# Layer 1's last stage of a two-layer graph and mixture-of-experts kernel: order of the expert-output loads, width of the sums, pieces of the last loads

## The chip, the cores and the metric

The kernel runs on one core of one Trainium2 chip. The metric is the device time of one execution in microseconds (us); of several executions the median is taken. The granted clock of TensorE in the profiled execution was 0.96 of full speed on average.

The engines are named as the profile names them: PE is TensorE's matmul, PEld its weight load, DVE is VectorE, ACT is ScalarE, POOL is GpSimd and SP is SyncE. In this kernel SP computes nothing: it issues most of the plain DMAs, in the order of its queue, and a DMA that has to wait for a semaphore holds all that stands behind it in that queue. POOL issues all indirect DMAs (gathers and scatters of rows).

## The reference, cut to what matters

There are 3327 rows of 256 values. Layer 0 is a graph step and a mixture of 16 experts; layer 1 is a graph step with attention and a mixture of 6 experts. The change lies in the end of layer 1's mixture:

```python
x = x + _L1_gnn_ref(_layernorm(x), adj, L1_gnn_W, L1_gnn_a)
x = x + _L1_ffn_ref(_layernorm(x), ...)

def _L1_ffn_ref(features, ...):
    rh = relu(features @ router_w1 + router_b1)
    expert_logits = softmax(rh @ router_w2 + router_b2)
    top_w, top_i = top_k(expert_logits, 2)
    routing_weights = softmax(top_w)
    h1 = relu(features . expert_w1 + expert_b1)      # 6 experts, 256 x 256
    h2 = relu(h1 . expert_w2 + expert_b2)
    expert_out = h2 . expert_w3 + expert_b3
    sel = take_along_axis(expert_out, top_i)
    return sum(sel * routing_weights[..., None])
```

So every row gets the sum of two weighted expert outputs, and this is added to the row itself.

## The kernel before, in words

The rows are cut into 26 row tiles of 128 rows; four row tiles make a chunk, and there are seven chunks (the last one has two tiles). `xs` holds all rows in SBUF as 128 x 26 x 256. The kernel computes each row only for its two experts. The routing writes, for each expert, a list of its rows into DRAM (`list1`); an entry has three words: the place of the output in `zd`, the number of the row in `hd`, and the weight.

Layer 1's experts are worked off in slots of 256 rows of one expert. There are usually 29 slots, 0 to 28 (`USUAL1`); more are behind a branch (`more`, L545) that is not taken here. `slots1` (L1290) is a software pipeline that Python writes out step by step. In step s it emits, in this order:

- `out1` of slot s-1 (L1254): eight matmuls, then y = acc + bias on DVE (L1262), then two multiplications by the row's weight (L1264), then `rows_out` (L602): two scatters of 128 rows each into `zd`, issued by POOL (L605).
- `weights_of` slot s+2 (L1277): the expert's weights are copied on DVE from `w1_all` into one of three tiles `w1s` (L1281).
- `places` up to slot s+4 (L567): a load of the slot's 256 list entries into `who` by SP (L572). There are 16 `who` tiles.
- `rows_in` up to slot s+3 (L575): two gathers of 128 rows each into `xg`, issued by POOL (L580). There are three `xg` tiles.
- `layer1` of slots s and s+1 (L1240), and `turned` of slot s+2 (L590): the transposes of `xg` on PE (L597).

`zd` has two rows of 256 values for every row: z holds a chunk's part of it as 128 x 4 x 2 x 256. The first four chunks (16 row tiles) are called `LOW`. Slots 0 to 22 (`LATE1` is 23) normally cover all rows of `LOW`; a flag, `early["low"]`, says on the chip whether they do. If so, the loads of z for `LOW` (`results`, L618, the load at L623) can go before the last slots are done; they wait for the scatters of slots 0 to 22 (`z_ready`). Before the change they are emitted one at a time in steps 23 to 26 (L1322), and the sums (`summed`, L629, one operation of 128 x 256 for each row tile and each of the two outputs, L633) and the store into `out` (`stored`, L635, from SP) three steps later (L1324 to L1326). In step 23 the load of z stands ahead of the list load of slot 28, which step 24 emits, because that is the order in which Python writes them.

After the slots come the remaining three chunks, of four, four and two row tiles (L1338 to L1341): one load each from SP, then the sums, and stores issued by ACT. These loads wait for all scatters. The last row tile has 127 rows and is stored in two pieces, 112 and 15 rows (L641).

The order within one engine is that of the program, as a scheduler of the tile framework has laid it out; `tc.issue_after(x)` makes what is in its block stand behind x in the order. `in_order()` (L553) does that for the last `who` load or other SP load of the slots. `last` keeps the instructions that such blocks refer to. DVE, POOL and SP work strictly in that order.

Of the kernel before, what the change touches and what calls it, by code (L numbers as in the profile page):

```python
# [15 lines left out]
OP = mybir.AluOpType  # L16
# [3 lines left out]
P = 128  # L20
# [5 lines left out]
def kernel(  # L26
# [26 lines left out]
    nc = tc.nc  # L53
    N, D = x.shape
    E0, _, H0 = ffn0_w1.shape
    E1, _, H1 = ffn1_w1.shape
# [5 lines left out]
    BT = 4  # L62
    CHUNKS = [list(range(t, min(t + BT, NT))) for t in range(0, NT, BT)]
# [25 lines left out]
    LATE1 = USUAL1 - E1  # L89
    LOW = CHUNKS[: 4 * len(CHUNKS) // 7]  # L90
# [26 lines left out]
    xs = keep.tile([P, NT, D], F32, name="xs")  # L117
# [123 lines left out]
    last = {}  # L241
# [311 lines left out]
    def in_order():  # L553

        return tc.issue_after(last["who"].ins) if "who" in last else nullcontext()

    def expert(table, s, E):

        with in_order():
            return (nc.sync.value_load(table[s : s + 1, 0:1], min_val=0, max_val=E - 1),  # L560
                    nc.sync.value_load(table[s : s + 1, 2:3], min_val=0, max_val=1))

    def load(tile_, source, which):
        e, new = which
        last["who"] = nc.sync.dma_start(tile_, source(bass.ds(e, 1)), cond=new, bounds_check="skip_entire_dma")

    def places(table, s, E, rows_of, size):  # L567

        who = io.tile([P, size // P, 3], I32, name="who", bufs=16)
        with in_order():  # L570
            at = nc.sync.value_load(table[s : s + 1, 1:2], min_val=0, max_val=E * NP)
        last["who"] = nc.sync.dma_start(who, rows_of[bass.ds(at, size), :].rearrange("(h p) w -> p h w", p=P))  # L572
        return who
# [28 lines left out]
    def rows_out(s, who, y):  # L602
        n = who.shape[1]
        for h in range(n):
            last["z"] = nc.gpsimd.indirect_dma_start(  # L605
                out=zviews[n * s + h], out_offset=bass.IndirectOffsetOnAxis(ap=who[:, h, 0:1], axis=0),
                in_=y[:, h, :], in_offset=None, bounds_check=2 * NP - 1, oob_is_err=False,
            )
            if s < LATE1:
                z_ready.append(last["z"].ins.name)  # L610

    def weight(who, h):

        return who.bitcast(F32)[:, h, 2:3]

    z_ready = []

    def results(blk, zp, low=None, z=None):  # L618

        n, t0 = len(blk), blk[0]  # L620
        z = zp.tile([P, BT, 2, D], F32, name="z") if z is None else z
        of, case = (zd, {}) if low is None else (zd_low, dict(cond=low, bounds_check="skip_entire_dma"))
        ins = nc.sync.dma_start(z[:, :n], of[2 * t0 * P : 2 * (t0 + n) * P, :].rearrange("(t p k) d -> p t k d", p=P, k=2), **case)  # L623
        if low is not None:
            for name in z_ready:
                tc.add_manual_dep(ins.ins, name, mybir.DependencyInfo(mybir.DependencyClass.Sync, mybir.DependencyReason.DATA))
        return z

    def summed(blk, z):  # L629

        for i, t in enumerate(blk):
            for k in range(2):
                nc.vector.tensor_tensor(z[:, i, 0, :], z[:, i, k, :], z[:, i, 0, :] if k else xs[:, t, :], op=OP.add)  # L633

    def stored(engine, blk, z):  # L635
        full = [t for t in blk if t < NF]
        engine.dma_start(
            out[full[0] * P : (full[-1] + 1) * P, :].rearrange("(t p) d -> p t d", p=P), z[:, : len(full), 0, :]
        )
# [292 lines left out]
    early = {}  # L932
# [28 lines left out]
    WB, BB = 3 * 2 * H1, 3 * 2 * H1 + D  # L961
# [108 lines left out]
    who = {}  # L1070
# [158 lines left out]
    w1s = [wts.tile([P, BB + 2 * 2], F32, name=f"v_{b}") for b in range(3)]  # L1229
# [7 lines left out]
    def weights1(s, i):  # L1237
        return w1s[s % 3][:, i * 2 * H1 : (i + 1) * 2 * H1].rearrange("p (k h) -> p k h", k=2)
# [15 lines left out]
    def out1(s, who, h2):  # L1254
        ps = bank(1 if s < EARLY1 else 0, [P, 2, D])
        w = weights1(s, 2)
        for h in range(2):
            for c in range(NC1):
                nc.tensor.matmul(ps[:, h, :], h2[:, c, h * P : (h + 1) * P], w[:, c, :],  # L1259
                                 start=(c == 0), stop=(c == NC1 - 1))  # L1260
        y = io.tile([P, 2, D], F32, name="y", bufs=4)
        last["dve"] = nc.vector.tensor_tensor(y, ps, w1s[s % 3][:, None, WB:BB].to_broadcast([P, 2, D]), op=OP.add)  # L1262
        for h in range(2):
            nc.vector.tensor_scalar(y[:, h, :], y[:, h, :], weight(who, h), None, op0=OP.mult)  # L1264
        rows_out(s, who, y)

    who = {}
# [17 lines left out]
    def table1_of(s):  # L1285
        return (early["table"], s) if s < EARLY1 else (table1, s - EARLY1)

    xg, xT, h1, h2, zs = {}, {}, {}, {}, {}

    def slots1(first, end):  # L1290
        for s in range(first - 3, end + 1):
            if first <= s - 1 < end:
                out1(s - 1, who[s - 1], h2.pop(s - 1))
            if first <= s + 2 < end:
                if s + 2 < EARLY1:
                    load(w1s[(s + 2) % 3], lambda e: w1d[e].rearrange("o p w -> p (o w)"), expert(*table1_of(s + 2), E1))
                else:
                    weights_of(s + 2)
            known = EARLY1 if s < EARLY1 - 2 else end
            for i in range(max(who, default=-1) + 1, min(s + 5, known)):  # L1300
                who[i] = places(*table1_of(i), E1, lists[1], S1)
            for i in range(max(xg, default=-1) + 1, min(s + 4, known)):
                xg[i] = rows_in(who[i], hd_of[0][: NE * P, :] if i < EARLY1 else hd[:, :])
            if first <= s < end:
                h2[s] = layer1(s, 1, h1.pop(s))
            if first <= s + 1 < end:
                h1[s + 1] = layer1(s + 1, 0, xT.pop(s + 1))
            if first <= s + 2 < end:
# [68 lines left out]
```

## Time and profile before

| what | value |
|---|---|
| time before, median of 3 runs | 1031.23 us (1025.27, 1031.23 and 1034.23) |
| the profiled execution, its own time | 1030.67 us |
| its span, from the first to the last instruction | 1028.9 us |
| PE busy | 929.3 us (90% of the span) |
| DVE busy | 497.6 us (48%) |
| POOL busy | 428.4 us (42%) |
| ACT busy | 260.8 us (25%) |
| busy PE in the window 954 to 977 us | 23.00 of 23.00 us |
| busy PE in the window 977 to 1003 us | 22.41 of 26.00 us |
| busy PE in the window 1003 to 1029 us | 1.56 of 26.00 us |

The profile is one execution. All times of its rows are counted from the start of the span. A row of the timeline has the start, the duration, the engine, the line of the kernel, the operation, what it writes and reads, how many instructions are merged into the row, and in brackets how long the engine stood idle before it and what ended that. "SPq", "POOLq" and "DVEq" are the sequencers of these engines: the issue of a DMA or a branch, which does not count as busy. A group's row has a count, a total of busy time and the mean of one in ns. The chain of work that ended last is followed back from the last instruction to what released each step.

In the timeline the 29 slots can be told by their y (L1262): those of slots 21 to 28 start at 962.91, 968.58, 974.26, 979.94, 985.62, 994.73, 1000.21 and 1004.63 us. The scatters of slot 22 are the two POOL rows that start at 974.18 and 975.49, those of slot 28 start at 1006.88 and 1008.15.

### The profile page before, as it was taken

The numbers are of one execution on the slowest core, as the hardware profiler recorded it, in microseconds if no ns is written. First come the engines' busy times: TensorE is split into PE (matmuls) and PEld (weight loads), VectorE is DVE, ScalarE is ACT, GpSimd is POOL, SyncE is SP. The second block draws the span as 40 slices with busy tenths as digits, with TensorE's granted clock in tenths as the row PEclk, the third lists the DMA queues.
The fourth block names the chain that finished last, engine by engine and source line by source line (L and its number), as shares of the span: only waits on it lengthen the run. The fifth ranks groups of instructions, "written<-read, shape, count | busy, mean of one in ns | idle before, by whom it ended". The sixth has DMA issues, their size and how long they took to land. (4 is left out here: it accounts for less than half of the span.)

```text
span 1028.9 us, 14333 instructions
## 1 busy us (share of the span) xinstructions
PE 929.3 (90%) x4505; PEld 782.0 (76%) x4505; DVE 497.6 (48%) x1824; ACT 260.8 (25%) x532; POOL 428.4 (42%) x408
## 2 busy tenths in 40 slices
PE   6889999859997999999999989999889588999980
PEld 5678888649886999888898777877668367888870
DVE  6565586225651222212223677658567442344663
ACT  3310302015321111111111443131132333444430
POOL 2040060632575345544544311005242476777741
PEclk9999999969998999999999999999999689999995
DMA  9989678457546575667788398867853955332375
GB/s 338 318 272 307 231 189 305 127 179 236 143 105 189 143 212 149 173 193 185 188 250 236 73 308 288 254 212 181 253 128 129 332 135 151 93 93 93 93 249 195
DMA packets 109634, 204.00 MB, mean 198 GB/s; under 512 B 31843, under 2 KB 64356, under 8 KB 109550
## 3 DMA queue, kind: packets, MB, share of 16 engines
q1 hardware_dynamic: 69952, 154.19, 47.3%
q0 software_dynamic: 20608, 30.69, 13.1%
q10 hardware_dynamic: 18990, 18.14, 5.9%
q8 instruction: 36, 0.59, 0.3%
q14 instruction: 48, 0.39, 0.1%
HBM read 173.74 MB, written 35.53 MB: 203 GB/s over the span
## 5 line engine op out<-in xcount | busy, mean ns | idle before, releaser
L797 PE MATMUL acc<-big,y 128*128 128x512 f32 (+2 forms) x1456 | 341.2, 389 | 28.3 <-DVE big L680 19.8
L797 PEld LDWEIGHTS acc<-big,y 128*128 128x128 f32 (+1 forms) x1456 | 264.3, 193 | 85.7 <-ACT y L853 9.2
L1027 PE MATMUL acc<-xT,w 128*128 128x256 f32 (+3 forms) x1024 | 212.8, 361 | 0.0
L1027 PEld LDWEIGHTS acc<-xT,w 128*128 128x128 f32 x1024 | 186.4, 198 | 15.9 <-issue 3.1
L363 POOL DMA_INDIRECT list<-where,t_idx x104 | 109.3, 1051 | 198.9 <-DVE t_idx L359 87.8
L680 DVE TENSOR_SCALAR big<-adj 128x1536 fp32r<-128x1536 int32 (+6 forms) x130 | 111.5, 860 | 121.3 <-DMA adj<-in_adj_t 78.2
L1056 POOL DMA_INDIRECT xd<-y,who x64 | 99.0, 1547 | 65.2 <-DVE y L1055 19.2
L1050 PE MATMUL acc<-w,hid 128*128 128x256 f32 (+3 forms) x512 | 118.0, 381 | 0.7 <-DVE x_out L439 0.7
L1002 POOL DMA_INDIRECT xg<-hd,who x64 | 63.2, 988 | 123.2 <-PE acc L1027 44.2
L1035 DVE TENSOR_TENSOR hid<-hid,acc 128x512 f32<-128x512 f32 (+3 forms) x64 | 40.1, 629 | 139.7 <-PE acc L1027 134.1
L1050 PEld LDWEIGHTS acc<-w,hid 128*128 128x128 f32 (+3 forms) x512 | 89.5, 178 | 20.7 <-issue 3.3
L1031 ACT ACTIVATE hid<-acc 128x512 f32<-128x512 f32 (+3 forms) x64 | 35.2, 550 | 202.6 <-PE acc L1027 195.9
L605 POOL DMA_INDIRECT zd<-y,who x58 | 70.2, 1210 | 25.2 <-DVE y L1264 14.3
L1250 ACT ACTIVATE h<-acc,v 128x256 f32<-128x256 f32 x116 | 55.0, 475 | 100.3 <-PE acc L1247 99.3
L580 POOL DMA_INDIRECT xg<-hd,who x58 | 57.9, 999 | 31.8 <-issue 15.8
L1247 PE MATMUL acc<-xT,v 128*128 128x256 f32 x232 | 63.5, 397 | 4.4 <-DMA v<-w1d 3.9
L1055 DVE TENSOR_SCALAR y<-acc,who 128x256 f32<-128x256 f32 x64 | 28.1, 478 | 71.7 <-PE acc L1050 68.0
L1262 DVE TENSOR_TENSOR y<-acc,v 128x512 f32<-128x512 f32 x29 | 20.1, 692 | 86.8 <-PE acc L1259 86.8
L1247 PE MATMUL acc<-h,v 128*128 128x256 f32 x232 | 61.3, 387 | 0.6 <-ACT h L1250 0.6
L268 POOL TENSOR_TENSOR ln_var<-ln_var,half 128x2 f32<-128x2 f32 (+2 forms) x19 | 15.2, 802 | 104.5 <-DVE ln_var L266 92.2
L1259 PE MATMUL acc<-v,h 128*128 128x256 f32 x232 | 56.7, 387 | 0.1
L1247 PEld LDWEIGHTS acc<-xT,v 128*128 128x128 f32 x232 | 44.6, 203 | 13.3 <-issue 4.2
(281 smaller groups left out, 926.7 us busy)
## 6 DMA issues: line engine op xcount, KB each, us to landing
adj<-in_adj_t SPq DMA_DIRECT2D x66, 768.0 KB, 6.4
w<-in_ffn_w SPq DMA_DIRECT2D x72, 512.0 KB, 5.8
adj<-in_adj_t SPq DMA_DIRECT2D x25, 639.5 KB, 6.0
adj<-in_adj_t SPq DMA_DIRECT2D x25, 512.0 KB, 4.3
v<-w1d SPq DMA_DIRECT2D x7, 898.0 KB, 10.5
hd<-ln_h ACTq DMA_DIRECT2D x12, 512.0 KB, 10.6
z<-zd SPq DMA_DIRECT2D x6, 1024.0 KB, 8.1
w_all<-w1d SPq DMA_DIRECT2D x6, 898.0 KB, 12.7
```

The lines of the kernel that those rows point to most:

```text
L363: ins = nc.gpsimd.indirect_dma_start(out=rows_of[2 * (t0 + j) + i], out_offset=bass.IndirectOffsetOnAxis(ap=idx[:, i, j : j + 1], axis=0), ...
L580: last["pool"] = nc.gpsimd.indirect_dma_start(out=xg[:, h, :], out_offset=None, in_=of, in_offset=bass.IndirectOffsetOnAxis(ap=who[:, h, 1 ...
L605: last["z"] = nc.gpsimd.indirect_dma_start(out=zviews[n * s + h], out_offset=bass.IndirectOffsetOnAxis(ap=who[:, h, 0:1], axis=0), in_=y[: ...
L680: last["mask"] = nc.vector.tensor_scalar(mask[:kr, :, :cols], a[:kr, :, :cols], value, None, op0=op)
L797: last["graph"] = nc.tensor.matmul(acc[c][k][:, :w], y[:kr, j, part, k * P : (k + 1) * P], mask[:kr, jj, i0 : i0 + w], start=(j == 0 and p ...
L1002: last["pool"] = nc.gpsimd.indirect_dma_start(out=xg[:m, h, :], out_offset=None, in_=hd_of[0][: NE0 * P, :] if s < HALF else hd[:, :], in_ ...
L1027: last["slot"] = nc.tensor.matmul(q[:, c, :n], w[:, k, h0 : h0 + 2 * P - 1 : 2], xT[:, k, :n], start=(k == 0), stop=(k == KD - 1))
L1050: nc.tensor.matmul(ps[:m, h, :], hid[c // 2][:, c % 2, h * P : h * P + m], w3[:, c // 2, c % 2, :], start=(c == 0), stop=(c == NC0 - 1))
L1056: ins = nc.gpsimd.indirect_dma_start(out=xd_of[2 + h] if s < USUAL0 else xd, out_offset=bass.IndirectOffsetOnAxis(ap=who[s][:m, h, 0:1], a ...
L1247: ins = nc.tensor.matmul(ps[:, c, :], w[:, k, c : H1 : NC1], src[:, k, :], start=(k == 0), stop=(k == 1))
L1250: last["act"] = nc.scalar.activation(dst[:, c, :], ps[:, c, :], AF.Relu, bias=w1s[s % 3][:, BB + 2 * i + c : BB + 2 * i + c + 1])
L1259: nc.tensor.matmul(ps[:, h, :], h2[:, c, h * P : (h + 1) * P], w[:, c, :], start=(c == 0), stop=(c == NC1 - 1))
```

## The change

It has three parts. All of them lie in the end of layer 1; two line offsets follow from it (L623 becomes L625, L633 becomes L635, L1262 becomes L1265).

1. The loads of z for `LOW` are emitted as two in step 24 and two in step 25, and not before the list load of slot 28. Each also waits for the y of the step's `out1` (`behind`), that is, for the last multiplication of slot 23's y (first two loads) and slot 24's (last two). `last["dve"]` is now that multiplication and not the addition before it.
2. A chunk's sums are two operations of 128 x 1024 and not eight of 128 x 256: first z's output 0 plus `xs`, then output 1 plus that. They are emitted for chunk 0 in step 25, for chunk 1 in step 26 and for chunks 2 and 3 in step 27, behind the weight copy and the y of that step.
3. The last three chunks are loaded, summed and stored in five pieces of two row tiles each, so the sums there are of 128 x 512.

On the engines the order changes as follows. SP's queue: the list load of slot 28 now stands right behind that of slot 27, and the four loads of z come behind it without anything between them. POOL's: the two gathers of slot 28 now stand ahead of the two scatters of slot 23, where they stood behind them; earlier, the scatters of slot 4 move ahead of the first gather of slot 8. DVE's: y of slot 24, weights of 27, sums of chunk 0, y of slot 25, weights of 28, sums of chunk 1, y of slot 26, sums of chunks 2 and 3, y of slots 27 and 28, and then the ten sums of the last pieces. Before, the sums of `LOW` were spread between the weight copy of slot 28 and y of slot 28. ACT's: seven stores at the end and not five. PE's order is the same.

```diff
-    def results(blk, zp, low=None, z=None):
-
-        n, t0 = len(blk), blk[0]
+    def results(blk, zp, low=None, z=None, behind=(), step=BT):
         z = zp.tile([P, BT, 2, D], F32, name="z") if z is None else z
         of, case = (zd, {}) if low is None else (zd_low, dict(cond=low, bounds_check="skip_entire_dma"))
-        ins = nc.sync.dma_start(z[:, :n], of[2 * t0 * P : 2 * (t0 + n) * P, :].rearrange("(t p k) d -> p t k d", p=P, k=2), **case)
-        if low is not None:
-            for name in z_ready:
-                tc.add_manual_dep(ins.ins, name, mybir.DependencyInfo(mybir.DependencyClass.Sync, mybir.DependencyReason.DATA))
+        for i in range(0, len(blk), step):
+            part = blk[i : i + step]
+            n, t0 = len(part), part[0]
+            ins = nc.sync.dma_start(z[:, i : i + n], of[2 * t0 * P : 2 * (t0 + n) * P, :].rearrange("(t p k) d -> p t k d", p=P, k=2), **case)
+            if low is not None:
+                for name in (*z_ready, *behind):
+                    tc.add_manual_dep(ins.ins, name, mybir.DependencyInfo(mybir.DependencyClass.Sync, mybir.DependencyReason.DATA))
         return z
 
     def summed(blk, z):
 
-        for i, t in enumerate(blk):
-            for k in range(2):
-                nc.vector.tensor_tensor(z[:, i, 0, :], z[:, i, k, :], z[:, i, 0, :] if k else xs[:, t, :], op=OP.add)
+        n, t0 = len(blk), blk[0]
+        for k in range(2):
+            nc.vector.tensor_tensor(z[:, :n, 0, :], z[:, :n, k, :], z[:, :n, 0, :] if k else xs[:, t0 : t0 + n, :], op=OP.add)
...
-        last["dve"] = nc.vector.tensor_tensor(y, ps, w1s[s % 3][:, None, WB:BB].to_broadcast([P, 2, D]), op=OP.add)
+        nc.vector.tensor_tensor(y, ps, w1s[s % 3][:, None, WB:BB].to_broadcast([P, 2, D]), op=OP.add)
         for h in range(2):
-            nc.vector.tensor_scalar(y[:, h, :], y[:, h, :], weight(who, h), None, op0=OP.mult)
+            last["dve"] = nc.vector.tensor_scalar(y[:, h, :], y[:, h, :], weight(who, h), None, op0=OP.mult)
         rows_out(s, who, y)
...
-            if not first and 0 <= s - LATE1 < len(LOW):
-                results(LOW[s - LATE1], tail, early["low"], zs[s - LATE1])
-            if not first and 0 <= s - LATE1 - 3 < len(LOW):
-                with tc.issue_after(last["copy"].ins):
-                    summed(LOW[s - LATE1 - 3], zs[s - LATE1 - 3])
-                stored(nc.sync, LOW[s - LATE1 - 3], zs.pop(s - LATE1 - 3))
-
+            for i in LOADED.get(s - LATE1, ()) if not first else ():
+                with in_order():
+                    results(LOW[i], tail, early["low"], zs[i], [last["dve"].ins.name])
+            for i in SUMMED.get(s - LATE1, ()) if not first else ():
+                with tc.issue_after(last["copy"].ins), tc.issue_after(last["dve"].ins):
+                    summed(LOW[i], zs[i])
+                stored(nc.sync, LOW[i], zs.pop(i))
+
+    LOADED, SUMMED = {1: (0, 1), 2: (2, 3)}, {2: (0,), 3: (1,), 4: (2, 3)}
...
-    zs = [(blk, results(blk, tail)) for blk in CHUNKS[len(LOW) :]]
+    zs = [(blk, results(blk, tail, step=2)) for blk in CHUNKS[len(LOW) :]]
     for blk, z in zs:
-        summed(blk, z)
-        stored(nc.scalar, blk, z)
+        for i in range(0, len(blk), 2):
+            summed(blk[i : i + 2], z[:, i : i + 2])
+            stored(nc.scalar, blk[i : i + 2], z[:, i : i + 2])
```

More of the change, by code (lines that the diff above doesn't have):

```diff
@@ L616 @@
     z_ready = []
-    def results(blk, zp, low=None, z=None):
-        n, t0 = len(blk), blk[0]
+    def results(blk, zp, low=None, z=None, behind=(), step=BT):
         z = zp.tile([P, BT, 2, D], F32, name="z") if z is None else z
         of, case = (zd, {}) if low is None else (zd_low, dict(cond=low, bounds_check="skip_entire_dma"))
-        ins = nc.sync.dma_start(z[:, :n], of[2 * t0 * P : 2 * (t0 + n) * P, :].rearrange("(t p k) d -> p t k d", p=P, k=2), **case)
-        if low is not None:
-            for name in z_ready:
-                tc.add_manual_dep(ins.ins, name, mybir.DependencyInfo(mybir.DependencyClass.Sync, mybir.DependencyReason.DATA))
+        for i in range(0, len(blk), step):
[5 more added lines that the diff above has]
+                    tc.add_manual_dep(ins.ins, name, mybir.DependencyInfo(mybir.DependencyClass.Sync, mybir.DependencyReason.DATA))
         return z
     def summed(blk, z):
-        for i, t in enumerate(blk):
-            for k in range(2):
-                nc.vector.tensor_tensor(z[:, i, 0, :], z[:, i, k, :], z[:, i, 0, :] if k else xs[:, t, :], op=OP.add)
+        n, t0 = len(blk), blk[0]
+        for k in range(2):
+            nc.vector.tensor_tensor(z[:, :n, 0, :], z[:, :n, k, :], z[:, :n, 0, :] if k else xs[:, t0 : t0 + n, :], op=OP.add)
     def stored(engine, blk, z):
         full = [t for t in blk if t < NF]
-        engine.dma_start(
-            out[full[0] * P : (full[-1] + 1) * P, :].rearrange("(t p) d -> p t d", p=P), z[:, : len(full), 0, :]
-        )
+        if full:
+            engine.dma_start(
+                out[full[0] * P : (full[-1] + 1) * P, :].rearrange("(t p) d -> p t d", p=P), z[:, : len(full), 0, :]
+            )
         for lo, hi in last_rows() if blk[-1] >= NF else ():
@@ L1320, in slots1 @@
                 early["more"] = asked(*table1_of(USUAL1))
-            if not first and 0 <= s - LATE1 < len(LOW):
-                results(LOW[s - LATE1], tail, early["low"], zs[s - LATE1])
-            if not first and 0 <= s - LATE1 - 3 < len(LOW):
-                with tc.issue_after(last["copy"].ins):
-                    summed(LOW[s - LATE1 - 3], zs[s - LATE1 - 3])
-                stored(nc.sync, LOW[s - LATE1 - 3], zs.pop(s - LATE1 - 3))
+            for i in LOADED.get(s - LATE1, ()) if not first else ():
[6 more added lines that the diff above has]
+    LOADED, SUMMED = {1: (0, 1), 2: (2, 3)}, {2: (0,), 3: (1,), 4: (2, 3)}
+    assert len(LOW) == 4 and max(SUMMED) < E1
     tail = ctx.enter_context(tc.tile_pool(name="tail", bufs=len(CHUNKS)))
```

## The prediction

> **What bounds the kernel now.** I read the windows first: PE is busy 23.00 of 23.00 us from 954 to 977, 22.41 of 26.00 from 977 to 1003 and 1.56 of 26.00 after that. So PE's work bounds the slots until 977; then something makes PE wait, and behind 1003 a chain without PE sets the end. The change touches only these two stretches (50 us). The waits of 975 to 1029 us name what PE lacked:
>
> ```profile
> POOL xg L580 <- DMA who<-list: 5.6, 1, 5.6
> PE mm L597 <- DMA xg<-hd,who: 2.9, 2, 2.5
> ```
>
> Columns: total us, times, longest. The list load of slot 28 comes late, so do its gathers, so PE stands 2.9 us. The timeline shows why:
>
> ```profile
> 977.30 0.98 POOL L605 DMA_INDIRECT zd<-y,who  x1 [0.30 <-issue]
> 978.58 0.97 POOL L605 DMA_INDIRECT zd<-y,who  x1 [0.30 <-issue]
> 978.64 0.37 SPq L623 DMA_DIRECT2D z<-zd  x1
> 979.27 0.37 SPq L572 DMA_DIRECT2D who<-list  x1
> ...
> 980.05 2.34 SPq L623 DMA_DIRECT2D z<-zd  x3
> ...
> 985.15 0.98 POOL L580 DMA_INDIRECT xg<-hd,who  x1 [5.59 <-DMA who<-list]
> ...
> 991.55 0.48 PE L597 MATMUL mm<-ident,xg 128*128 128x128 f32 x2 [2.49 <-DMA xg<-hd,who]
> ```
>
> The list load stood in SP's queue behind the first z load, which waited for slot 22's scatters, and then behind its 1024 KB in the DMA queue. y of slot 25 starts at 985.62 and y of slot 26 at 994.73: 9.11 us, where the slots before take 5.68 each. The loss is 3.43 us.
>
> A second loss, in POOL's rows near the end:
>
> ```profile
> 1001.78 3.51 POOL L605 DMA_INDIRECT zd<-y,who  x1 [2.98 <-DVE y L1264]
> ...
> 1005.60 0.97 POOL L605 DMA_INDIRECT zd<-y,who  x1 [0.31 <-DVE y L1262]
> 1006.88 0.97 POOL L605 DMA_INDIRECT zd<-y,who  x1 [0.30 <-issue]
> 1008.15 0.98 POOL L605 DMA_INDIRECT zd<-y,who  x1 [0.31 <-issue]
> ```
>
> Slot 27's first scatter takes 3.51 us against 0.97; the three after it queue up. The chain that ended last then goes through the last scatter and the last z loads:
>
> ```profile
> 1008.15 3.75 DMA zd<-y,who
> ...
> 1012.24 5.94 DMA z<-zd
> ...
> 1018.27 2.64 DVE z L633 x8
> 1020.96 2.17 DVE z L633 x7
> ```
>
> From 1018.27 DVE sums without a pause to 1025.07; a load that is out at 1012.24 lands 5.94 us later.
>
> **The change part by part.** The sum is made against the profiled execution: span 1028.9, own time 1030.67, 0.56 under the median 1031.23.
>
> *1. The list load ahead of the z loads.* Slot 28's list load follows slot 27's, which was out before 940 (SP's rows from 940 on begin with the z load at 978.64). The buffer it refills is slot 12's, long done. Its gathers stand on POOL behind slot 22's scatters, so at 977.30 and 978.58, 7.85 us earlier; with 2.8 us to land (the DMA page's median near there) they are there by 982.4, and PE asks at 988.9. The stall goes: -3.43 us. y's operands from slot 26 on are ready at 991.3, 996.5 and 1001.2. Slot 23's scatters go 2.6 us later; no early z load waits for them, the last loads wait for far later ones, and POOL, with no more gathers to issue, has caught up by slot 25. Earlier, slot 4's scatters pass slot 8's first gather (866.63 to 869.19); its second gather stays at 870.49 and PE takes both at 875.25 without a wait: nothing.
>
> *2. The z loads.* SP holds the first for slot 22's scatters as before: 978.64. Slot 23's y, the added wait, ended at 975.6: nothing. The second follows 0.5 to 1 us later; the last two wait for slot 24's y, 981.28, and went out near 981 and 982 before. Behind them in SP's queue are only the stores. So the landings stay, about 984.3 (before the list load behind it, which POOL had by 985.15), 987.25 (980.05 and 7.2 us to landing), 990 (between), 993.7 (982 and 11.7).
>
> *3. The wide sums.* No row has 128x1024. A 128x256 addition takes 421 ns alone and every 0.337 us in a row (6.73 us for 20 in 1018 to 1025); y's 128x512 takes 692 ns. The slope is 271 ns for 256, so I estimate 1.23 us for 1024. The second of a pair must wait for the first (before, another tile stood between), so a chunk costs 2.5 us against 2.7: bounds 2.2 (full overlap) and 2.7 (no gain). DVE's new order, with what waits:
> - sums 0 stand behind slot 27's weight copy (ends 982.6), wait for the first landing, 984.3, and end at 986.8. Queued behind are slot 25's y (ready 985.62, ends 988.2) and slot 28's weight copy (ends 989.5). PE needs that copy at 992.0 (995.39 in the timeline, less 3.43): 2.5 us to spare.
> - sums 1: 989.5 to 992.0. y 26: ready 991.3, ends 993.4.
> - sums 2 and 3: the last landing 993.7; four operations, end about 998.1. y 27, ready 996.5, ends 999.5; y 28 starts when ready, at 1001.2.
> So each y from 25 to 27 is late, by 0.7 to 1.6 us; their scatters have time, and the late sums are no longer beside slot 27's scatter.
>
> *4. POOL's end.* Slot 27's scatters run from about 999.5 to 1001.7, so slot 28's start as soon as weighted: 1001.2 + 0.73 + 0.35 + 0.28 = 1002.55, the second at 1003.83 instead of 1008.15. That is 4.32 us with the 3.43 in it, so the queue gives 0.89. The bound below: the 3.51 comes again on slot 27, 2.54 us, and slot 28's second scatter starts at about 1005.9; then this part and the first give 2.2 in all.
>
> [...]
>
> *5. The pieces.* Counted from the first z load's issue: before, 1024 KB land at 5.94, the next at 8.6 (12.73 and 8.1 later), the last 512 KB, by the GB/s of 2 us windows (45, 325, 330, 384, 227), at about 9.95. The same rates put the first 512 KB at 4.35 (adj's 512.0 KB loads: 4.3), the others at 5.95, 7.3, 8.6, 9.95. A piece's sums are two dependent 128x512: 2 x 0.69 + 0.08 = 1.46 against 1.35. DVE runs 4.45 to 5.9, then from 6.05 on without a pause: four pieces, to 11.9, against 12.83: -0.9. Then ACT's stores: before, the 128-row store was issued ahead of the last sums (1024.77 against 1025.07); now all three come behind: +0.45. Net -0.5. The two more loads and stores are issued (0.4 us each) beside the sums. Bounds: -1.1 (overlapped sums) and +0.95 (first piece no earlier than 5.94).
>
> Sum: -3.43 - 0.89 - 0.5 = -4.8 us. Own time 1025.9, span 1024.1, against the median 1031.23: **1026.4**. The bounds of the parts give -1.3 (2.2 less 0.95) to -5.4 (4.32 and 1.1).
>
> **The rivals.**
> - *DVE or POOL takes up half of it.* The last early landing comes 3.5 us later (997.2, so that y 27 ends at 1002 and its scatters push slot 28's), or a scatter of slot 27 is held like that at 1001.78: either way slot 28's second scatter starts 2.1 us later, at 1005.9. For it: the 3.51 us row, which the profile doesn't explain. Against: only one such row, and DVE has nothing left to do beside slot 27's scatters. 1026.4 + 2.1 = 1028.5.
> - *Slower: sums 0 hold DVE.* Place: slot 25's y and slot 28's weight copy wait behind a z load. With a landing at T the copy ends at T + 5.2 and PE pays from T = 986.8 on; at 986.8 + 4.8 = 991.6 all is eaten. If the loads share the queue so that all land with the last, at 993.7, it costs 6.9: 1033.3. For it: four loads are in flight together. Against: they landed one after another, 987.25 to 993.7, and POOL had the small load behind the first by 985.15.
> - *Pieces that don't overlap.* Five loads of 4.3 us in a row take 21.5 where 9.95 did: about 11.5 slower, 1038. The landings of before overlap, 2.7 us apart for 1024 KB, and speak against it. [...]
> - *It doesn't do what it says:* slot 28's gathers come no earlier, 1031. The order on SP and POOL speaks against it.
>
> **How the numbers follow.** Forecast 0.65 (its own range 1024 to 1028, before the scatter of runs); half of it 0.18; sums hold DVE 0.07; serial pieces 0.03; nothing 0.04; more than the sum, 1020 to 1024, 0.03. The three runs before spread over 9 us, so a median of three may lie 2.5 us off. The range is 1021.5 to 1031.5: it holds forecast, half and nothing with that scatter and leaves out the slower rivals. A measurement of this kernel can tell about 1% (10.3 us) from no change. Faster by over 1% needs less than 1020.9: 0.06, from the scatter and the last case. Slower by over 1% needs more than 1041.5: 0.03. Within 1%: 0.91.
>
> **What would show it.** No wait of PE for xg near 989 and 5.7 us between the y of slots 25 and 26; slot 28's gathers at 977.3; sums 0 before y 25; no scatter over 1.6 us behind 999; the second scatter of slot 28 near 1003.8; first piece landed 4.3 us after its issue, DVE done 11.9 after it. I am wrong if slot 28's weight copy makes PE wait, if y 28 starts later than its operands, or if the pieces land together.

## The result, and the profile after

| what | before | after |
|---|---|---|
| median, 20 runs each | 1030.74 us | 1021.68 us |
| lowest and highest of them | 1019.63 to 1038.19 | 1014.14 to 1028.81 |
| the profiled execution, its own time and span | 1030.67, 1028.9 | 1028.81, 1026.3 |
| start of slot 22's y in it | 968.58 | 972.25 |

The ratio of the times is 0.9935, with a 95% interval from 0.9906 to 0.9964. Of 1030.74 us that is 6.7 us less, from 3.7 to 9.7; the two medians themselves lie 9.06 us apart. The forecast was 4.8 us less.

Two executions of one and the same kernel reach slot 22 up to 16 us apart (three profiles of before: 955.61, 968.58, 971.38), for reasons upstream of the change. The profiled execution of after is also the slowest of its 20. So single spans can't be compared. In what follows I use **the stretch**: from the start of slot 22's y to the start of the last instruction that the profile shows, 0.05 us before the end of the span. It is 60.26 us in the profile of before and 53.97 in that of after; a second profile of after and one of its variant without pacing (e7 below) gave 54.01 both.

The waits after 975 us, in the profile after (columns: total us, times, longest):

```profile
DVE z L635 <- DMA z<-zd: 11.7, 2, 9.3
POOL zd L605 <- DVE y L1267: 8.1, 6, 3.5
...
PE acc L1250 <- ACT h L1253: 0.6, 1, 0.6
```

PE's wait for `xg` and POOL's for `who` are gone from the list. The timeline after, for SP, POOL, DVE and PE:

```profile
980.96 0.98 POOL L580 DMA_INDIRECT xg<-hd,who  x1 [0.30 <-issue]
982.24 0.98 POOL L580 DMA_INDIRECT xg<-hd,who  x1 [0.30 <-issue]
982.32 3.67 SPq L625 DMA_DIRECT2D z<-zd  x4
...
988.78 1.23 DVE L635 TENSOR_TENSOR z<-z,xs 128x1024 f32<-128x1024 f32 x1 [2.48 <-DMA z<-zd]
990.04 1.23 DVE L635 TENSOR_TENSOR z<-z 128x1024 f32<-128x1024 f32 x1
991.19 0.68 DVE L1265 TENSOR_TENSOR y<-acc,v 128x512 f32<-128x512 f32 x1
...
992.56 0.64 PE L597 MATMUL mm<-ident,xg 128*128 128x128 f32 x4
992.72 1.09 DVE L1284 COPY v<-w_all 128x1796 f32 x1 [0.20 <-issue]
...
997.37 2.35 DVE L635 TENSOR_TENSOR z<-z,xs 128x1024 f32<-128x1024 f32 x2
997.47 1.96 POOL L605 DMA_INDIRECT zd<-y,who  x1 [1.68 <-DVE y L1267]
999.74 1.96 POOL L605 DMA_INDIRECT zd<-y,who  x1 [0.30 <-DVE z L635]
...
1003.26 0.97 POOL L605 DMA_INDIRECT zd<-y,who  x1 [1.56 <-DVE y L1267]
...
1007.49 0.98 POOL L605 DMA_INDIRECT zd<-y,who  x1 [0.30 <-issue]
1011.57 2.45 SPq L625 DMA_DIRECT2D z<-zd  x5
```

Slot 28's gathers go out at 980.96 and 982.24, which is 8.7 and 10.0 us behind slot 22's y; before it was 16.6 and 17.9. PE transposes them at 992.56 without a wait. Chunk 0's sums stand ahead of slot 25's y, which starts at once behind them, and slot 28's weight copy (992.72) ends at 993.81; PE uses it at 995.62, so 1.8 us are to spare. Slot 26's scatters (997.47, 999.74) take 1.96 us each beside the wide sums, but POOL then stands idle for 1.56 us before slot 27's, so that is absorbed. The chain that ended last now reads (start, us, what):

```profile
1007.49 3.75 DMA zd<-y,who
...
1011.57 3.80 DMA z<-zd
...
1015.47 0.70 DVE z L635
...
1021.61 0.69 DVE z L635
```

It goes through the same steps, but the first piece lands 3.80 us after its issue and DVE is done 10.73 us after it (12.83 before).

One part of this chain is not what its name says. The rows of the last scatter have landed at 1009.78, 2.29 us after its start (2.29 before, too). The rest of its 3.75 us goes to the branch `more` (L549) that is not taken: POOL waits there for its own scatters and then spends 1.24 us in one instruction, to 1011.30, and the trace has the semaphores that SP's loads wait for set near the end of it, by 1011.25:

```profile
L549 POOLq INC_SWDGE_SEM x1: 1235/1235/1235, 1010.1 to 1010.1; - x1
```

The change leaves this part alone, so the third column of the next table is the same in nearly all rows.

### The profile page after: what moved, and what is told of

Same layout as the page of the kernel before. It is cut to its first block, busy times and chain, and to the rows that moved or that the text cites. A ratio compares the mean times of both kernels' runs of the same rounds, so it can differ in the third digit from the quotient of the medians.

```text
span 1026.3 us, 14305 instructions
## 1 busy us (share of the span) xinstructions
PE 930.8 (91%) x4505; PEld 783.3 (76%) x4505; DVE 495.9 (48%) x1790; ACT 260.6 (25%) x532; POOL 429.9 (42%) x408
## 5 line engine op out<-in xcount | busy, mean ns | idle before, releaser
L1053 PEld LDWEIGHTS acc<-w,hid 128*128 128x128 f32 (+3 forms) x512 | 89.6, 178 | 19.6 <-issue 3.3
L605 POOL DMA_INDIRECT zd<-y,who x58 | 70.4, 1214 | 26.7 <-DVE y L1267 16.6
L1265 DVE TENSOR_TENSOR y<-acc,v 128x512 f32<-128x512 f32 x29 | 20.0, 691 | 80.7 <-PE acc L1262 77.6
L1262 PE MATMUL acc<-v,h 128*128 128x256 f32 x232 | 56.3, 385 | 0.1
```

What stands on the lines that cost most here:

```text
L605: last["z"] = nc.gpsimd.indirect_dma_start(out=zviews[n * s + h], out_offset=bass.IndirectOffsetOnAxis(ap=who[:, h, 0:1], axis=0), in_=y[: ...
L1053: nc.tensor.matmul(ps[:m, h, :], hid[c // 2][:, c % 2, h * P : h * P + m], w3[:, c // 2, c % 2, :], start=(c == 0), stop=(c == NC0 - 1))
```

## The experiments

Each row is one profiled execution, cut at four marks: slot 28's y, its second scatter, the first of the last z loads, and the end of the stretch. All are in us, the first column from the start of slot 22's y. The rows without an e are the two kernels.

| kernel | y 28 | to its 2nd scatter | to the last loads | to the end | stretch |
|---|---|---|---|---|---|
| before | 36.05 | 3.52 | 4.08 | 16.61 | 60.26 |
| e11_before_again | 40.36 | 2.63 | 4.08 | 16.49 | 63.56 |
| e13_before_third | 35.16 | 3.52 | 4.09 | 16.63 | 59.40 |
| after | 32.61 | 2.63 | 4.08 | 14.65 | 53.97 |
| e12_after_again | 32.61 | 2.74 | 4.08 | 14.58 | 54.01 |
| e4_list_first | 32.61 | 5.05 | 4.08 | 16.44 | 58.18 |
| e1_loads_only | 32.61 | 5.04 | 4.08 | 16.53 | 58.26 |
| e2_wide_only | 38.76 | 2.63 | 4.09 | 16.31 | 61.79 |
| e3_pieces_only | 36.87 | 3.52 | 4.08 | 14.59 | 59.06 |
| e5_narrow | 33.77 | 3.93 | 4.09 | 14.21 | 56.00 |
| e7_no_pace | 32.62 | 2.63 | 4.08 | 14.68 | 54.01 |
| e8_sums_last | 32.62 | 3.62 | 7.07 | 15.46 | 58.77 |
| e9_ones | 32.62 | 2.63 | 4.08 | 14.31 | 53.64 |
| e10_zero_last | 39.60 | 5.18 | 4.09 | 14.49 | 63.36 |

My theory was that of the prediction: the position of slot 28's list load makes PE wait, the long scatter costs at POOL's end, the pieces shorten the last stretch. The rivals: the pacing or the wide sums do it, the sums hold DVE, or the pieces don't overlap.

**e4_list_first: the old kernel, only slot 28's list load one step earlier.**

```diff
-            for i in range(max(who, default=-1) + 1, min(s + 5, known)):
+            for i in range(max(who, default=-1) + 1, min(s + (6 if first == 0 and s == LATE1 else 5), known)):
```

> The kernel before with one edit: the list load of slot 28 stands ahead of the first z load in SP's queue. Loads of z, sums and tail as before. I read the end stretch, from the start of slot 22's y to the end of the span: 60.3 us before, 54.1 after the change. Theory (the list load behind the z load is the cause of PE's stall, and the change gains 3.4 us by it, 0.9 in POOL's queue and 1.9 in the last pieces): PE's wait for xg is gone, slot 27's and 28's y are ready 3.4 us earlier, the stretch is 56.0 to 56.9. Rival (the stall comes from the z loads' traffic on the DMA queues, which the change paces): the wait stays at least in half, the stretch is over 58.5.

Measured: stretch 58.18. PE's wait is gone and y 28 stands where after has it, 3.44 us earlier than in the profile of before. So the order of these two loads on SP is the cause of the stall; this step of the theory stands. But the stretch lies 1.3 us above the range expected. POOL's timeline in e4 tells why:

```profile
996.15 4.86 POOL L605 DMA_INDIRECT zd<-y,who  x1 [3.31 <-DVE y L1264]
1001.31 3.84 POOL L605 DMA_INDIRECT zd<-y,who  x1 [0.30 <-DVE z L633]
1005.45 1.01 POOL L605 DMA_INDIRECT zd<-y,who  x1 [0.31 <-DVE y L1264]
```

Both scatters of slot 26 are held beside the narrow sums, 4.86 and 3.84 us where 0.97 is usual. Those of slots 27 and 28 queue up behind them, and slot 28's second starts 5.05 us after its y where after needs 2.63. Of the 3.44 us that PE gained, 1.5 (5.05 less 3.52) are lost again at POOL.

**e1_loads_only: part 1 alone** (`results` with `behind`, the loads in steps 24 and 25, `last["dve"]` moved; the sums narrow and in their old steps, the last loads whole).

```diff
-            if not first and 0 <= s - LATE1 < len(LOW):
-                results(LOW[s - LATE1], tail, early["low"], zs[s - LATE1])
+            for i in {1: (0, 1), 2: (2, 3)}.get(s - LATE1, ()) if not first else ():
+                with in_order():
+                    results(LOW[i], tail, early["low"], zs[i], [last["dve"].ins.name])
```

> Part 1 of the change alone: the z loads of the first four chunks as in the change (behind all list loads, two by two, paced by y), sums narrow and at their old steps, the last three chunks whole. Theory: as with the list load moved alone, the end stretch 56.0 to 56.9 us. Rival (pacing the loads by y is worth something of its own): under 55.5; or (it costs, since the loads are later) over 57.5.

Measured: 58.26, and missed in the same way: slot 26's scatters took 4.52 and 4.17 us. The number lies in the range of the rival that the later loads cost something, but e4, which doesn't pace them, agrees within 0.09 us in every column. So in this stretch what part 1 does is the order on SP's queue, and the pacing shows no effect.

**e2_wide_only: part 2 alone** (`summed` as in the change, in the old steps).

```diff
-        for i, t in enumerate(blk):
-            for k in range(2):
-                nc.vector.tensor_tensor(z[:, i, 0, :], z[:, i, k, :], z[:, i, 0, :] if k else xs[:, t, :], op=OP.add)
+        n, t0 = len(blk), blk[0]
+        for k in range(2):
+            nc.vector.tensor_tensor(z[:, :n, 0, :], z[:, :n, k, :], z[:, :n, 0, :] if k else xs[:, t0 : t0 + n, :], op=OP.add)
```

> Part 2 alone: the kernel before with a chunk's sums as two operations. Theory: PE's stall stays (2.9 us of waiting for xg), the last chunks' sums take 6.2 us instead of 6.7, and slot 27's first scatter is held by one wide sum at most (about 2 us instead of 3.5): end stretch 58.5 to 60.3. [...]

Measured: 61.79, more than expected, but for a reason that isn't the sums: y 28 came at 38.76, since the granted clock fell to 0.5 behind PE's wait (see e11). No scatter took over 1.97 us, where about 2 were expected at most. Behind y 28 the last part is 16.31, against 16.49 to 16.63 in the three profiles of before. The 2.63 to the second scatter alone shows nothing: e11, with narrow sums, has the same. POOL's timeline of e2:

```profile
985.26 1.96 POOL L605 DMA_INDIRECT zd<-y,who  x1 [0.31 <-DVE z L633]
...
994.75 1.96 POOL L605 DMA_INDIRECT zd<-y,who  x1 [4.98 <-DVE y L1264]
997.02 1.97 POOL L605 DMA_INDIRECT zd<-y,who  x1 [0.31 <-DVE z L633]
```

The three scatters beside wide sums took 1.96 or 1.97 us, and none took more.

**e3_pieces_only: part 3 alone** (five pieces, their sums narrow).

```diff
-    zs = [(blk, results(blk, tail)) for blk in CHUNKS[len(LOW) :]]
+    zs = [(blk, results(blk, tail, step=2)) for blk in CHUNKS[len(LOW) :]]
```

> Part 3 alone: the kernel before with the last three chunks loaded, summed and stored in five pieces, sums narrow. Theory: the first piece lands 3.8 us after the first issue instead of 5.9, the end comes 1.5 to 2.1 us earlier, the end stretch is 58.2 to 58.8. Rival (pieces gain nothing, the gain there came from the wide sums): 59.8 to 60.8.

Measured: 59.06, above the 58.2 to 58.8 expected, again with the clock fallen for 3.4 us (y 28 at 36.87, 0.8 later than in before). The last part is 14.59 against 16.61: the pieces alone give 2.0 us, four times what was predicted for them, and the wide sums add nothing to it there (14.65 in after). If anything they cost a little in the last part: with narrow sums it is 14.59 here and 14.21 in e5.

**e5_narrow: the changed kernel with narrow sums.**

> The change with narrow sums (128x256) in the same places of DVE's order. New theory, after the list load moved alone gave only 2.1 of 3.4 us (slot 26's scatters took 4.86 and 3.84 us beside runs of narrow sums): a scatter that starts just after a sum is held until the run of sums ends, and wide sums let it in after one. Expected: slot 26's first scatter, which starts beside the 16 narrow sums of chunks 2 and 3, takes 3 to 6 us; the end stretch (from slot 22's y to the end, 54.0 after the change) is 54.5 to 57. Rival (the width is nothing, the change's order of sums alone frees the scatters): no scatter over 2.1 us, stretch 53.7 to 54.3.

Its edit puts the removed lines of e2's diff back. Measured: 56.00, inside the expected size, but not by the mechanism: no scatter was held for long here, as the rival had it. POOL's timeline of e5:

```profile
988.16 1.16 POOL L605 DMA_INDIRECT zd<-y,who  x1 [2.44 <-DVE y L1267]
989.63 1.04 POOL L605 DMA_INDIRECT zd<-y,who  x1 [0.30 <-issue]
994.78 0.97 POOL L605 DMA_INDIRECT zd<-y,who  x1 [4.11 <-DVE y L1267]
```

Instead POOL waited 4.11 us for slot 27's weighted rows: the first z load went out 1.3 us later than in after (11.37 against 10.07), and the sixteen narrow sums of chunks 2 and 3 (5.4 us) stand ahead of slot 27's y, which started at 32.52 instead of 29.67. So y 28 came 1.16 later too. The later load isn't due to the edit: e11, the kernel before, has the same 11.37. The landings tell the two causes apart. From the landing of chunk 0 DVE works almost without a pause to slot 27's y, and that takes 13.15 us in after, e12 and e9, though chunk 0 landed at 16.52, 16.94 and 16.79 there; in e5 it landed at 17.97 and the same work took 14.55. So of the 2.85 us by which slot 27's y came later, 1.45 are the landing and 1.40 the narrow sums.

**e8_sums_last: the changed kernel with the sums of chunks 2 and 3 behind slot 28's y.**

```diff
-    LOADED, SUMMED = {1: (0, 1), 2: (2, 3)}, {2: (0,), 3: (1,), 4: (2, 3)}
+    LOADED, SUMMED = {1: (0, 1), 2: (2, 3)}, {2: (0,), 3: (1,), 6: (2, 3)}
```

> The change with the sums of chunks 2 and 3 behind slot 28's y instead of ahead of slot 27's. Theory (scatters are held beside sums): slot 26's and 27's scatters take 0.97 to 1.1 us, slot 27's y is no longer late, but slot 28's two scatters now stand beside wide sums and take about 2 us each, so the last z loads start 1 to 2 us later than after the change: stretch 55 to 56. Rival (scatters are held by something else, the sums only happen to be near): slot 28's scatters take 0.97, stretch 53.7 to 54.3.

Measured: 58.77, well above 55 to 56. The scatters of slot 28 were held as the theory said; from the timeline of e8:

```profile
993.27 1.97 POOL L605 DMA_INDIRECT zd<-y,who  x1 [2.45 <-DVE y L1267]
995.54 1.96 POOL L605 DMA_INDIRECT zd<-y,who  x1 [0.30 <-DVE z L635]
996.68 1.51 SPq L640 DMA_DIRECT2D out_x<-z  x2
1002.60 2.49 SPq L625 DMA_DIRECT2D z<-zd  x5
```

That costs 1.0 us up to the second scatter's start. But the last loads then go out 7.07 us later instead of 4.08, of which the second scatter's own hold is 1.0. The other 2 us weren't in the expectation. The trace shows what they are made of. The second scatter landed 4.51 us after its start instead of 2.29. Of these 2.2 us its hold is 1.0; why the other 1.2 came is not shown, but the two stores into `out` were in flight beside it. And SP, which stands at the branch L549 ahead of the loads, waits there for the semaphores of these two stores. SP's waits in e8 from 990 to 1004 us have the row:

```profile
SPq L549 <- SPq L549: 3.5, 3, 2.1
```

The longest of these waits ends at 1001.88, when the second store (out at 997.82) has landed. POOL had set its semaphores by 1001.52, so SP's wait costs 0.8 us. The sums of `LOW` have no good place behind slot 28's y.

**e10_zero_last: the changed kernel with chunk 0 loaded last, its sums still ahead of slot 25's y.** This tests the slower rival.

```diff
-    LOADED, SUMMED = {1: (0, 1), 2: (2, 3)}, {2: (0,), 3: (1,), 4: (2, 3)}
+    LOADED, SUMMED = {1: (1, 2), 2: (3, 0)}, {2: (0,), 3: (1,), 4: (2, 3)}
...
-        nc.vector.tensor_tensor(y, ps, w1s[s % 3][:, None, WB:BB].to_broadcast([P, 2, D]), op=OP.add)
+        with tc.issue_after(last["sum"].ins) if "sum" in last else nullcontext():
+            nc.vector.tensor_tensor(y, ps, w1s[s % 3][:, None, WB:BB].to_broadcast([P, 2, D]), op=OP.add)
```

> The change with chunk 0 loaded as the last of the first four chunks, and its sums kept ahead of slot 25's y as in the change. It tests the slower rival of the prediction: DVE held by a z load that lands late. Theory: chunk 0 lands at 25.2 us after slot 22's y, slot 28's weight copy ends at about 30.3, PE needs it at 23.4, PE waits 6.5 to 7.5 us; the stretch is 60 to 63 (longer if TensorE's clock drops after the wait). Rival (DVE's lateness is covered elsewhere): under 57.

Measured: 63.36. The timeline of e10:

```profile
991.92 1.23 DVE L635 TENSOR_TENSOR z<-z,xs 128x1024 f32<-128x1024 f32 x1 [10.32 <-DMA z<-zd]
...
994.33 0.68 DVE L1266 TENSOR_TENSOR y<-acc,v 128x512 f32<-128x512 f32 x1
...
995.07 2.08 PE L1262 MATMUL acc<-v,h 128*128 128x256 f32 x4 [2.45 <-DVE y L1266]
...
997.00 1.36 PEld L1250 LDWEIGHTS acc<-xT,v 128*128 128x128 f32 x4 [0.58 <-DVE v L1285]
```

DVE stands for 10.32 us before the load, and PE stands behind DVE's y and then its weight load behind the weight copy. Slot 28's copy ends at 29.57 instead of 21.57 us after slot 22's y; PE had 1.8 us to spare, so 6.2 us should reach it. It used the copy 6.25 later, and y 28 came 7.0 later, with the clock at half for 6.8 us in between. The mechanism of the rival is real; it didn't come about because the loads land one after another (at 16.52, 19.64, 22.50 and 25.17 us in after). The 5.18 us behind y 28 is a side effect of the edit: slot 27's weighting came behind slot 28's addition on DVE (its scatter started at 40.83).

**e11_before_again and e13_before_third: the kernel before, unchanged, profiled twice more.**

> The kernel before, unchanged, for one more profile. In the profiles of part 2 alone and part 3 alone TensorE's granted clock fell to 0.5 for 6.8 and 3.4 us right behind PE's wait for slot 28's rows, which lengthened these stretches by 2.7 and 0.8 us; in the profile of before it did not fall there. Theory (that fall follows the wait in some executions, so on average the change gains more than 3.4 us by taking the wait away): the stretch is 60.3 without a fall and 61 to 63.5 with one. Rival (the fall belongs to those two kernels): 60.1 to 60.5 and no fall.

> The kernel before, for a third profile. Theory (PE's wait for slot 28's rows is there each time, a fall of the granted clock right behind it most times): stretch 60.3 without a fall, 61 to 63.6 with one.

Measured: 63.56 and 59.40. The stall is no constant: y 28 stands at 36.05, 40.36 and 35.16 in the three profiles. It follows the list load of slot 28, which went out at 10.69, 12.00 and 9.89; so e13 stayed below the 60.3 expected without a fall of the clock. In e11 PE stood 4.21 us, and then its matmuls ran slowly. The timeline of e11, and the row of the windows that holds it (the last three columns are granted clock, DMA share and GB/s):

```profile
980.29 0.67 PE L597 MATMUL mm<-ident,xg 128*128 128x128 f32 x2 [4.21 <-DMA xg<-hd,who]
981.54 0.70 PE L597 MATMUL mm<-ident,xg 128*128 128x128 f32 x2 [0.57 <-DMA xg<-hd,who]
982.03 3.62 PE L1259 MATMUL acc<-v,h 128*128 128x256 f32 x8
```

```profile
980.00:985.00 5.00, 4.14 (x11) 3.14 (x12) 0.00 (x0) 0.59 (x1) 1.81 (x2) 0.50 0.60 218
```

The profile of before has the same eight matmuls behind its stall, in 1.89 us:

```profile
992.80 1.89 PE L1259 MATMUL acc<-v,h 128*128 128x256 f32 x8
```

The granted clock fell to 0.5 for 3.4 us (e3) or 6.8 us (e2, e10, e11) near the end of PE's waits or right behind them, in four of the six profiles that have such a wait. In this stretch it stayed at 1.00 in before and e13 until PE's work was done. Of the eight profiles without such a wait, that of after shows 1.00 in all windows from 940 to 1005 us, and y 28 stands at 32.61 or 32.62 us in seven. The length of the waits alone doesn't tell the two cases apart: in before PE waited 2.49 and 0.43 us and the clock stayed; in e3 it waited only 1.02 and 1.08 us, with a pair of transposes between, and the clock fell:

```profile
984.25 0.48 PE L597 MATMUL mm<-ident,xg 128*128 128x128 f32 x2 [1.02 <-DMA xg<-hd,who]
985.80 0.70 PE L597 MATMUL mm<-ident,xg 128*128 128x128 f32 x2 [1.08 <-DMA xg<-hd,who]
```

In e13 the waits were 1.03 and 1.00 us and it didn't fall. What decides stays open.

**e12_after_again and e7_no_pace: the changed kernel again, and without the wait for y.**

```diff
-                for name in (*z_ready, *behind):
+                for name in z_ready:
```

> The change, unchanged, for one more profile. Theory (without PE's wait nothing in the stretch depends on the clock's fall, and the scatters of slots 27 and 28 stand beside no sums): the stretch is 53.5 to 54.6 again. Rival (the stretch after the change varies as before's did, 60.3 and 63.6): outside of that.

> The change without the added wait of the z loads for y. Theory (the pace is neutral): the last two of the four loads are issued about 1 us earlier, sums 2 and 3 end no later, slot 28's y starts when its operands are ready: stretch 53.5 to 54.6. Rival (the pace keeps the z loads out of the gathers' way): PE waits for slot 28's rows, stretch over 55.

Measured: 54.01 and 54.01. After repeats within 0.04, where the three profiles of before differ by 4.2. Without the pacing the four loads go out at 9.28, 9.97, 10.65 and 11.60, and nothing that counts moves; it costs nothing and gives nothing here.

**e9_ones: the changed kernel with the last chunk in two pieces of one row tile.**

```diff
-    zs = [(blk, results(blk, tail, step=2)) for blk in CHUNKS[len(LOW) :]]
+    zs = [(blk, results(blk, tail, step=len(blk) // 2)) for blk in CHUNKS[len(LOW) :]]
```

> The change with its last piece of two row tiles cut into two of one row tile (six loads, sums and stores at the end). The last piece lands 9.2 us after the first load's issue, and 4.8 us go by from there to the end of the span. Theory (the end is bound by the landing of the last piece plus its sums and three stores): one tile's two sums take 0.9 us instead of 1.4, and the 128-row store goes out earlier: the end stretch falls from 54.0 to 53.0 to 53.5. Rival (a sixth load and the more dependent sums cost what they gain): 53.8 to 54.3. Against the kernel before, by the stretches of before known so far (60.3 and 63.6): 7 to 10 us less, ratio 0.990 to 0.993.

Its sums and stores go by the same pieces, in the order of the pieces. Measured: median 1021.38 us over 12 runs against 1027.8 of before (17 runs), ratio 0.9923 with an interval from 0.9893 to 0.9952. The stretch is 53.64, between the 53.0 to 53.5 of the theory and the 53.8 to 54.3 of the rival. It is 0.33 and 0.37 us shorter than in the two profiles of after, most of it in the last column. Against before it is faster; against after the intervals overlap, so that it beats it rests on the stretch alone.

## Why the prediction came out as it did

**The number.** The forecast was 1026.4 us, and the measured median, 1021.68, lies 4.7 us below it. It stands just inside the range of 1021.5 to 1031.5, in the band from 1020 to 1024 to which the prediction gave a chance of 0.03. The direction and the parts were right, but that the range holds the median is owed to the room it left for the scatter of runs: the -6.29 us of the pair of profiles lies beyond the -5.4 that the bounds of the parts allowed.

**Part 1, PE's stall: right in the mechanism and in the profiled size, too small on average.** Against the profile of before, y 28 moved by 3.44 us, where 3.43 were predicted. What the working left out is that the stall is not always the one of that profile. Over the five profiles with the old order of the list load (before, e11, e13, e2, e3) y 28 stands at 37.44 on average, and at 32.61 or 32.62 in the seven with the new order and a DVE that holds nobody back: 4.83 us. PE's waits for the rows are no longer on average than in before (in the order named 2.9, 4.8, 2.0, 2.9 and 2.1 us in all), so the 1.4 us on top are, by an estimate from these numbers, nearly all the clock of 0.5 in e11, e2 and e3.

**Parts 2 and 3, the early loads and the wide sums: right in the order, with landings up to 1.1 us too early.** The first three landings were predicted 15.7, 18.7 and 21.4 us behind slot 22's y and came at about 16.5, 19.6 and 22.5; the fourth at 25.2 against 25.1. A pair takes 2.48 us where it stands alone, against 2.5 (one operation takes 1.22 to 1.23, as estimated). The y of slots 25 and 26 started 1.9 and 1.2 us later than the earliest in the other profiles with the new order (17.03 in e4 and 22.71 in e7), so they are 4.94 us apart and not 5.7; the spare time of slot 28's weight copy was 1.8 instead of 2.5.

**Part 4, POOL's end: the sum is right, the working leaves out a hold.** The second scatter of slot 28 moved by 4.33 us (4.32 predicted, with the 3.43 in it), and slot 27's scatters took 0.97 as predicted. But the 0.89 in it isn't there in every execution of before: the column is 3.52 in two of the three profiles and 2.63 in e11, as in after. And the working has no hold for slot 26's scatters, which took 1.96 us each beside wide sums, 1 us more than alone. All 15 scatters that started some 0.1 us into a wide sum (in after, e2, e7, e8, e9, e10 and e12) took 1.96 or 1.97 us and ended 0.84 to 0.87 us after the end of that sum. Two scatters of before that stand beside narrow sums look as if nothing held them:

```profile
989.51 1.03 POOL L605 DMA_INDIRECT zd<-y,who  x1 [0.30 <-issue]
990.84 1.01 POOL L605 DMA_INDIRECT zd<-y,who  x1 [0.30 <-DVE z L633]
```

They fit the same figure: they started 0.25 us into a sum of 0.41 and ended 0.87 and 0.85 us after its end. The hold costs nothing at the end in after: each of slot 26's scatters got through behind one sum and not behind all four, and slot 27's rows were weighted later than POOL was ready (it stood idle for 1.56 us).

I also had the role of the width wrong. I gave 0.89 us to the queue and credited it to the place of the sums. E4 and e1 show that with the list load moved and the sums left narrow, the holds grow to 4 to 5 us and slot 28's second scatter comes 2.4 us later than in after. So part 1 alone takes only 2.1 or 2.0 us off the stretch of before: the change of the sums is what lets it count. Whether it is their width or their new places is only half settled: e2 (wide, old places) has no long hold, e5 (narrow, new places) has none either, and with narrow sums in old places before, e1, e3, e4 and e13 have one or two and e11 has none. Over all profiles 5 of the 11 scatters that started about 0.1 us into a narrow sum were held for the rest of the run of sums, and none of the 15 beside wide ones. That speaks for the width. The run that would settle it, the list load moved with wide sums in their old places, was not made.

**Part 5, the pieces: the mechanism right, the term of the sum mis-sized.** Predicted -0.5, measured 16.61 to 14.65, -1.96. The landings were predicted at 4.35, 5.95, 7.3, 8.6 and 9.95 us and came at 3.80, 5.16, 6.51, 7.86 and 9.22: 0.55 to 0.8 earlier. A pair of sums comes every 1.33 to 1.37 us, not 1.46, so that DVE keeps pace with the landings, 1.35 apart, and ends at 10.73 instead of 11.9. The stores behind it cost 0.15 (3.92 against 3.77 from DVE's end to the end) and not 0.45. All three errors point the same way: by an estimate from these rows about 0.7 us are the landings, 0.5 the pace of the sums and 0.3 the stores. My bound below, -1.1, left the first landing at its estimate and varied only the sums.

**The sum.** In the pair of profiles: -3.44, -0.89 and -1.96 make -6.29 (60.26 to 53.97). With the average stall, 4.83 in place of 3.44, it is -7.7; that takes the 0.89 for granted, and the plain averages, 61.07 over the three profiles of before and 53.99 over the two of after, differ by 7.1. The interval of the measured -6.7, from -9.7 to -3.7, holds all of these, and the predicted -4.8 as well.

**The rivals.** *Half of it* did happen, but in e4 and e1, not in after: DVE's sums took up 2.4 us of POOL's end where the sums stayed narrow. *Slower, sums 0 hold DVE*: its mechanism is shown by e10; its condition, all loads landing together, didn't hold. *Pieces that don't overlap*: no; halves land 1.35 us apart, which is 388 GB/s (524288 bytes in 1.35 us). *It doesn't do what it says*: no; the gathers of slot 28 come 7.9 us earlier against slot 22's y.

What stays open: why a scatter beside narrow sums is now and then held for the whole run of them. In e13 one that started 96 ns into a sum took 1.17 us, and another at 97 ns 3.52:

```profile
998.20 1.17 POOL L605 DMA_INDIRECT zd<-y,who  x1 [2.97 <-DVE y L1264]
...
1003.68 3.52 POOL L605 DMA_INDIRECT zd<-y,who  x1 [2.97 <-DVE y L1264]
```

## What to carry to other kernels

A small load that feeds a later stage doesn't belong behind a large one that has to wait, in a queue like SP's here: the list load's 3 KB came 5.6 us late for POOL in before and PE stood for 2.9 us, and with the one load moved ahead (e4) y 28 came 3.44 us earlier. The engine that it starves may pay a second time in granted clock: it fell to 0.5 for 3.4 or 6.8 us in three of the five profiles with the late list load. A freed engine doesn't shorten the end by itself: look at what the queue behind it then runs beside (in e4 scatters of 4.86 and 3.84 us beside short sums, so that the stretch lost 2.1 us and not 3.44). And for a last load that nothing hides, smaller pieces paid here: the five landed 1.35 us apart, DVE kept pace with a pair of sums every 1.33 to 1.37 us, and the last part fell by 2.0 us.

## What the runs showed of the hardware that I had not expected

- The 15 scatters that started some 0.1 us into a 128x1024 sum on DVE took 1.96 or 1.97 us, where 0.97 is usual, and ended 0.84 to 0.87 us after the end of that sum. Beside back-to-back 128x256 sums a scatter took 1.01 to 1.17 us, or was held on for 3.5 to 4.9 us.
- Around a wait of PE of 2 to 5 us in all, the granted clock fell to 0.5 for 3.4 or 6.8 us in four profiles and not in two: in e2 and e11 eight matmuls took 3.62 us instead of the 1.89 of before.
- In the profile of after the first 512 KB of a queued series landed 3.80 us after its issue and each further one 1.35 us later. The last of five such halves landed at 9.22 us, the last of the three whole loads of before at 9.92, so halving cost nothing here.
- The last scatter's rows landed 2.29 us after its start, but the loads behind it went out only after 4.08, since POOL's waits at a branch that isn't taken lie between.
